# Two FNO attention layers on one core: one mixing of the images per pass, and every unit of work issued in one written-out order

## The chip, the cores and the metric

One core of a Trainium2 chip. TensorE (PE in the profile) multiplies, VectorE (DVE), ScalarE (ACT) and GpSimd (POOL) do elementwise work, and SyncE (SP) issues transfers. The metric is the time of one launch in microseconds on the device.

## The reference

The input is `x` of shape (2, 56, 128, 128): two images b of 56 channel planes each. Two layers of the same form follow each other, `x = x + layer(gn(x))`. Cut to what matters:

```python
xn = inorm(xa)                                  # xa: 112 single planes
k, q, v = (spectral_conv(xn, w) + skip1x1(xn)) for 8 heads each
attn = softmax(q k^T / 128, over the 56 planes of the image)
out  = spectral_conv(attn v) + skip1x1(attn v)  # heads folded to one plane
att  = inorm(out + xa)
h = gelu(inorm(spectral_conv(inorm(att))) + skip(...))
h = inorm(spectral_conv(h)) + skip(h)
y = inorm(h) + att
```

`spectral_conv` keeps 2 x 16 rows by 16 columns of the 2-D Fourier transform. Planes stay 128 x 128. Scores, values and heads are therefore computed among 512 modes per plane, and only three things touch whole planes: the statistics and transforms of the input, the hidden image under the Gelu, and the output. The part of every layer that is linear and pointwise is a 56 x 56 mixing of the raw planes of an image.

## The kernel before, in words

Both images' raw planes are held in `X2` (128 partitions: 56 planes twice, for two interleaved halves of the rows, plus pad partitions). For each layer L and image b a pass has these steps:

- `turned` (lines 356 to 373): a unit of 8 row pairs is transposed by TensorE into a pair of PSUM banks (L363 in layer 0, L365 in layer 1, there on 120 partitions at once), copied out by ACT (L368, L371) into the plane tile `P[b]`, and DVE takes `bn_stats` (L373). Eight units make an image.
- `modes_chain` (L458 on): group statistics, `Sqrt` on ACT (L468), reciprocal, then the plane is scaled and shifted in place (L479 on ACT, L481 on DVE) before the Fourier matmuls (L485) and `to_modes` (L386). A transfer over SP's queue moves half of the modes to other partitions (L505).
- `gram` (L521), `gram_chain`, `scale_x` (L560: `X2` times the group scale, in place, DVE alone), `scores` (L607, L588), `softmax_chain`, `values` (L630), `mix_chain` (the 56 x 56 mixing matrix `BTx`), `heads` (L700).
- `norms_chain`: closed-form norms (Sqrt on ACT, L731), the spectrum `Z` of the hidden image, and two scaled copies of the mixing matrix, `Bs` and `Be`.
- `gelu`: for each of four parts A of an image, `synthesis` (L761) of the spectrum into two PSUM pairs and `mixed` (L776, with `Bs`) on top of it; ACT applies the Gelu (L829), DVE takes `bn_stats` (L831), TensorE transposes (L811), ACT copies (L812), forward transform (L799), DVE copy (L804).
- `h_chain`: four in-place DVE transposes (L845), `to_modes`, norms (Sqrt, L869, L876), spectrum of the output.
- `end`: for each part synthesis and `mixed` again (L776, with `Be`); DVE adds the hidden image (L926), POOL adds the raw image (L928), which SP's queue loaded again (L906); in layer 0 the sum goes to `X2` and to a DRAM tile `store`, and is turned for layer 1; in layer 1 it goes to `out`.

The order of the work is written by generators: each step is a generator that yields an estimated cost, and `_woven(lead, *bulks)` fills the waits of a chain of small steps (the lead) with units of another image's bulky step. PSUM comes from two pools, two single banks (`bank`) and three pairs (`pair`), taken in turn. The framework (Tile) makes each engine's order from this one, and may set an instruction ahead of an earlier one; an engine then works through its instructions in order and waits by semaphores.

`prepare` (L235 on) makes coefficient matrices from the weights: for layer 0 first on DVE and POOL (`prepare(0, V, G)`), for layer 1 on POOL. `relay` and `build` (L341) spread them into the tiles `WU`, `WT`, `WM`.

Of the kernel before, what the change touches and what calls it, by code (L numbers as in the profile page):

```python
# [16 lines left out]
HEADS = 8  # L44
EPS = 1e-5

# [3 lines left out]
for _name, _n in (  # L50
    ("ident", N), ("fw", 32), ("fh", N), ("gw", N), ("group", N), ("dup", N), ("ext", N), ("fold", 64),
    ("raw", 56), ("count", 2), ("syn", 1), ("same", 32), ("m8", 8), ("m16", 16), ("n2", 1), ("fx", N), ("gh", 2 * N),
):
    _PARTS[_name] = (sum(n for _, n in _PARTS.values()), _n)
N_CONST = sum(n for _, n in _PARTS.values())


def _constants():
# [9 lines left out]
    at = 4 * (pos % 32) + pos // 32  # L68
    fh = over_h(at)[0]
    g, s, e, c = at // 16, at // 8 % 2, at // 2 % 4, at % 2  # L70
    by_layer = []
    for hx, hz in (
        (16 * g + 8 * c + 4 * s + e, pos.reshape(4, 4, 2, 4).transpose(1, 0, 3, 2)),
        (16 * g + 4 * c + 8 * s + e, pos.reshape(4, 2, 4, 4).transpose(2, 0, 3, 1)),
    ):
        z = over_h(hz.reshape(-1))[1]
        by_layer += [over_h(hx)[0], np.concatenate([z, z], 0).reshape(N, 2 * N)]
# [7 lines left out]
    for r in range(2):  # L85
# [20 lines left out]
        "ident": np.eye(N), "fw": fw, "fh": fh, "gw": gw, "group": group, "dup": dup, "ext": ext,  # L106
        "fold": fold, "raw": raw,
# [7 lines left out]
    whole = np.concatenate([parts[n] for n in _PARTS if n in parts] + by_layer, 1)  # L115
    return {"all": np.ascontiguousarray(whole, np.float32)}

# [23 lines left out]
def _woven(lead, *bulks):  # L141

    rest = chain(*bulks)
    for want in lead:
        while want > 0:
            cost = next(rest, None)
            if cost is None:
                break
            yield cost
            want -= cost  # L150
    yield from rest


def _with(bulk, extra):

    for cost in bulk:
        next(extra, None)
        yield cost


def _run(units):
    for _ in units:
        pass
# [3 lines left out]
def fno_layers(ctx: ExitStack, tc: tile.TileContext, x, out, weights, small, const):  # L167
    nc = tc.nc
    V, S, G, T = nc.vector, nc.scalar, nc.gpsimd, nc.tensor
    pool = lambda name, bufs, **kw: ctx.enter_context(tc.tile_pool(name=name, bufs=bufs, **kw))  # L170
    cp = pool("const", 1)
    xp = pool("x", 1)
    pp = pool("plane", 1)
    wp = pool("mats", 1)
    sp = pool("modes", 1)
    sm = pool("small", 1)
    dp = pool("dram", 1, space=bass.MemoryType.DRAM)
    ps = pool("psum", 2, space=bass.MemoryType.PSUM)
    pq = pool("pair", 3, space=bass.MemoryType.PSUM)

    def bank():
        return ps.tile([N, 512], F32, name="bank")

    def pair():
        return pq.tile([N, 2, 512], F32, name="pair")

    def little(name, shape):
        return sm.tile(shape, F32, name=name)
# [3 lines left out]


    Ct = cp.tile([N, N_CONST], F32, name="C")
    C = {k: Ct[:, o : o + n] for k, (o, n) in _PARTS.items()}
    ident = C["ident"]
    nc.scalar.dma_start(out=ident, in_=const["all"][:, :N])
    stage = cp.tile([N, 1632], F32, name="stage")
    nc.scalar.dma_start(out=stage[:, :1088], in_=weights[0].rearrange("p m r n t -> p (m r n t)"))
    smt = [cp.tile([N, N_SMALL], F32, name=f"sm{n}") for n in range(2)]  # L200
    for n in range(2):
        nc.scalar.dma_start(out=smt[n], in_=small[n : n + 1, :].to_broadcast([N, N_SMALL]))
    nc.scalar.dma_start(out=Ct[:, N:], in_=const["all"][:, N:N_CONST])
    X2 = xp.tile([N, B, 64, N], F32, name="X2")
    xin = x.rearrange("b k (g c r) w -> c b k g (r w)", c=2, r=8)
    for b in range(B):
        for g in range(0, 8, 2):
            for c in range(2):
                nc.sync.dma_start(
                    out=X2[64 * c : 64 * c + K, b, 8 * g : 8 * g + 16, :].rearrange("p (g r) w -> p g (r w)", r=8),  # L210
                    in_=xin[c, b, :, g : g + 2, :],
                )
    for b in range(B):
        nc.sync.dma_start(out=X2[K:64, b], in_=x[b, :8, :64, :])
    eps = cp.tile([N, 1], F32, name="eps")
    V.memset(eps, EPS)
    ones = cp.tile([N, N], F32, name="ones")
    V.memset(ones, 1.0)
    P = [pp.tile([N, 8192], F32, name=f"P{b}") for b in range(B)]
    plane = [t[:, : N * K].rearrange("p (i k) -> p i k", i=N) for t in P]  # L220
    WU = wp.tile([N, 4096], F32, name="WU")
    WT = wp.tile([N, 4096], F32, name="WT")
    WM = wp.tile([N, 1024], F32, name="WM")
# [5 lines left out]
    hT = [WT[:, 2048 + 896 * j : 2944 + 896 * j].rearrange("p (r e c k) -> p r e c k", r=2, e=4, c=2) for j in range(2)]  # L229
    xr = cp.tile([N, 3, 1024], F32, name="xr")  # L230
    G.memset(xr.rearrange("p a b -> p (a b)"), 0.0)
    store = dp.tile([B, K, N, N], F32, name="store")


    def prepare(layer, first, second):  # L235

        sml = smt[layer]
# [6 lines left out]
        der = little(f"der{layer}", [N, 48])  # L244
# [8 lines left out]
        tt, ts = second.tensor_tensor, second.tensor_scalar  # L253
        ss, vp = col("ss", 8), col("vp", 8)
        tt(ss, par["s_q"], par["s_k"], ALU.mult)
        tt(vp, par["s_p"], par["s_v"], ALU.mult)
        g2 = col("g2")
        tt(g2, par["g1"], par["g1"], ALU.mult)
        ts(col("score_g", 8), ss, g2, 1.0 / N, ALU.mult, ALU.mult)
        ts(col("mix", 8), vp, par["g1"], None, ALU.mult)  # L260
        tt(col("A0"), par["g2"], par["gan"], ALU.mult)
        tt(col("A02"), d["A0"], d["A0"], ALU.mult)
        tt(col("A0m0"), d["A0"], par["m0sw"], ALU.mult)
        ts(col("gan2"), par["gan"], par["gan"], EPS, ALU.mult, ALU.add)
        ts(col("dc0"), par["m0sw"], par["b2"], par["m0sb"], ALU.mult, ALU.add)
        tt(col("bb"), par["ban"], par["bmo"], ALU.add)
        tt(col("gm1"), par["gmo"], par["m1sw"], ALU.mult)
        tt(col("m12"), par["m1sw"], par["m1sw"], ALU.mult)
        tt(col("m2"), par["m1sw"], par["m1sw"], ALU.add)
        first.tensor_tensor(Wf, Wf, _bc(rawc[:, 0], 1, 2 * N_W), ALU.mult)  # L270
        first.tensor_tensor(M, M, _bc(rawc[:, 1:3], 2, N_W), ALU.mult)
        first.tensor_tensor(W, W, M, ALU.add)
        first.tensor_tensor(W[:, 0, 0:32, :], W[:, 0, 0:32, :], _bc(sml[:, 0:32], 2, 8), ALU.add)
# [5 lines left out]
        def place(e, t64, to, re, im, k):  # L279
# [4 lines left out]
            e.tensor_tensor(u, re, m0, ALU.mult)  # L284
            e.tensor_tensor(v, im, m1, ALU.mult)
            e.tensor_tensor(to[:, :, 0], u, v, ALU.subtract)
            e.tensor_tensor(u, im, m0, ALU.mult)
            e.tensor_tensor(v, re, m1, ALU.mult)
            e.tensor_tensor(to[:, :, 1], u, v, ALU.add)

        def product(e, room, o, a, b, conj, minus, scale, k):
            t64 = [room[:, 64 * n : 64 * n + 64].rearrange("p (a t) -> p a t", a=8) for n in range(4)]
            re, im, u = t64[:3]
            e.tensor_tensor(re, part(0, a), part(0, b), ALU.mult)
            e.tensor_tensor(u, part(1, a), part(1, b), ALU.mult)
            e.tensor_tensor(re, re, u, ALU.add if conj else ALU.subtract)
            e.tensor_tensor(re, re, _bc(minus, 2, 8), ALU.subtract)
            e.tensor_tensor(im, part(0, a), part(1, b), ALU.mult)
            e.tensor_tensor(u, part(1, a), part(0, b), ALU.mult)
            e.tensor_tensor(im, im, u, ALU.subtract if conj else ALU.add)  # L300
            for t in (re, im):
                e.tensor_scalar(t, t, scale, None, ALU.mult)
            place(e, t64, cpt[:, o : o + 16].rearrange("p (a c) t -> p a c t", c=2), re, im, k)
            return t64

        product(first, rooms[0], 0, 1, 0, True, ss, g2, 3)
        t64 = product(second, rooms[1], 16, 3, 2, False, vp, par["g1"], 5)
        place(
            second, t64, cpt[:, 32:36].rearrange("p (n c) t -> p n c t", c=2), W[:, 0, 32:34, :], W[:, 1, 32:34, :], 5,
        )  # L310
        tcs = little("tc", [N, 8, 36])
        return par, d, cpt, tcs

    def relay(cpt, tcs, room, groups):

        L = room.rearrange("p (t e c j s) -> p t e c j s", t=8, e=2, c=2, j=4)
        for o, n in groups:
# [17 lines left out]
            S.copy(tcs[:, :, o : o + n], pt[:, : 8 * n].rearrange("p (t n) -> p t n", t=8))  # L335
            yield 0.0

    def build(to, tcs, o, ts):

# [695 lines left out]
```

## Time and profile before

| | us |
|---|---|
| runs of the kernel before | 554.09, 555.94 (median), 558.58 |
| span of the profiled execution (one of its own; the page gives no total time for it) | 548.9 |
| PE busy | 440.6 |
| DVE busy | 350.6 |
| ACT busy | 189.6 |
| POOL busy | 180.4 |

A row of the groups reads: line, engine, operation, output tile from input tiles, partitions by elements, count, then busy time of the group in us and the mean of one in ns, then the idle time of the engine just before these instructions with what ended it. A row of the stretches gives, for a stretch from A to B us, the busy time of each engine with the count of instructions, the granted TensorE clock as a share of full speed, the busy share of the DMA engines and the rate in GB/s. A row of the timeline or of the chain begins with start and duration in us.

### The profile page before, as it was taken

Reading aid. Unit: us, or ns where it says so; the run is one execution under the profiler, and the core shown is the slowest. Engines: PE = TensorE matmul, PEld = TensorE weight load, DVE = VectorE, ACT = ScalarE, POOL = GpSimd, SP = SyncE. Lnnn points to the kernel's source line nnn. Section 1 sums busy time; section 2 is a strip of 40 time slices with the busy share of each in tenths; the row PEclk is TensorE's granted clock in tenths of the full one; section 3 lists DMA queues with packets and bytes.
Section 4 is the critical chain, followed back from the end, with each engine's and each line's share of the span. In section 5 each row is a group of like instructions: output and inputs, shape, how many; then the busy total and the mean of one; then the engine's idle time right before and its main releaser. Section 6 shows DMA issues by size and latency. Waiting matters only on the chain.

```text
span 548.9 us, 14430 instructions
## 1 busy us (share of the span) xinstructions
PE 440.6 (80%) x6438; PEld 296.4 (54%) x6438; DVE 350.6 (64%) x593; ACT 189.6 (35%) x238; POOL 180.4 (33%) x198
## 2 busy tenths in 40 slices
PE   2548879899989999789688948899998999977480
PEld 1423748768675555445563447577775555534340
DVE  0575579934547676869459994761636867767670
ACT  2333232064545557142102313224546457502000
POOL 2460325900082000155366771440000000044484
PEclk9998797999998999996667958989998999979696
DMA  8992000050000000065144641121000000027597
GB/s 209 220 221 28 10 2 11 7 148 3 2 3 1 1 2 1 1 198 172 51 132 117 187 116 32 13 69 41 4 1 2 1 1 3 1 60 225 181 219 289
DMA packets 18477, 41.00 MB, mean 75 GB/s; under 512 B 4704, under 2 KB 5472, under 8 KB 18400
## 3 DMA queue, kind: packets, MB, share of 16 engines
q1 hardware_dynamic: 17696, 38.71, 26.0%
q10 hardware_dynamic: 720, 1.38, 1.0%
q8 instruction: 50, 0.82, 0.6%
q14 instruction: 11, 0.09, 0.1%
HBM read 24.68 MB, written 14.68 MB: 72 GB/s over the span
## 4 chain that ended last, share of the span: by engine, by line
PE 46%; DVE 30%; ACT 8%; issue 7%; POOL 4%; DMA 3%; POOLq 1%; ACTq 0%; DVEq 0%
PE pair L776 8%; PE pair L761 5%; PE pair L811 5%; DVE X L560 4%; DVE stats L373 4%; PE bank L521 4%; PE bank L700 3%; DMA C<-const_all 3%; DVE P L926 3%; PE bank L485 3%; PE bank L588 3%; PE bank L799 2%; DVE WT L406 2%; PE bank L386 2%; POOL P L928 2%
## 5 line engine op out<-in xcount | busy, mean ns | idle before, releaser
L926 DVE SCALAR_TENSOR_TENSOR P<-P,hs,pair 128x1024 f32<-128x1024 f32 x32 | 40.0, 1268 | 18.8 <-PE pair L776 18.8
L831 DVE BATCH_NORM_STATS2 stats<-P 128x6 f32<-128x512 f32 x64 | 40.5, 680 | 17.3 <-ACT P L829 17.1
L928 POOL TENSOR_TENSOR X<-P,xr 128x1024 f32<-128x1024 f32 x16 | 39.3, 2462 | 32.1 <-DVE P L926 20.2
L373 DVE BATCH_NORM_STATS2 stats<-P 128x6 f32<-128x448 f32 x64 | 35.7, 612 | 20.9 <-ACT P L371 10.6
L560 DVE TENSOR_TENSOR X<-X,gvr 120x1024 f32<-120x1024 f32 x32 | 49.0, 1560 | 0.0
L829 ACT ACTIVATE P<-pair 128x1024 f32<-128x1024 f32 x32 | 32.6, 1026 | 33.0 <-PE pair L776 32.4
L521 PE MATMUL bank<-P 128*64 128x56 f32 (+1 forms) x1024 | 40.5, 250 | 0.0
L776 PE MATMUL pair<-X,Be 57*64 57x512 f32 x256 | 40.1, 726 | 0.0
L521 PEld LDWEIGHTS bank<-P 128*64 128x64 f32 (+1 forms) x1024 | 38.9, 164 | 2.2 <-issue 1.9
L395 POOL MEMSET WT<- 128x256 f32 x4 | 1.3, 314 | 114.5 <-PE bank L799 88.8
L811 PEld LDWEIGHTS pair<-C,P 120*128 120x128 f32 x256 | 27.3, 145 | 21.3 <-issue 11.5
L776 PE MATMUL pair<-X,Bs 57*64 57x512 f32 x256 | 38.4, 641 | 0.0
L761 PE MATMUL pair<-C,WT 32*128 32x128 f32 x512 | 29.3, 336 | 11.1 <-DVE P L926 5.3
L761 PEld LDWEIGHTS pair<-C,WT 32*128 32x128 f32 x512 | 24.0, 229 | 23.4 <-issue 9.3
L811 PE MATMUL pair<-C,P 120*128 120x120 f32 x256 | 35.2, 281 | 0.1
L341 POOL TENSOR_TENSOR WT<-tc,C 128x1024 f32<-128x1024 f32 x8 | 26.5, 3343 | 20.1 <-ACT tc L335 11.0
L812 ACT COPY WT<-pair 128x896 f32<-128x896 f32 x32 | 28.8, 905 | 11.8 <-PE pair L811 11.5
L363 PE MATMUL pair<-C,X 56*128 56x56 f32 x256 | 17.4, 291 | 17.5 <-DMA X<-x 11.9
L371 ACT COPY P<-pair 128x896 f32<-128x896 f32 x16 | 14.4, 901 | 45.7 <-PE pair L365 45.7
L363 PEld LDWEIGHTS pair<-C,X 56*128 56x128 f32 x256 | 14.9, 197 | 24.0 <-DMA X<-x 10.0
L365 PE MATMUL pair<-C,X 120*128 120x120 f32 x128 | 20.3, 312 | 9.2 <-POOL X L928 9.2
L365 PEld LDWEIGHTS pair<-C,X 120*128 120x128 f32 x128 | 16.1, 163 | 21.2 <-POOL X L928 11.6
(260 smaller groups left out, 880.2 us busy)
## 6 DMA issues: line engine op xcount, KB each, us to landing
X<-x SPq DMA_DIRECT2D x16, 448.0 KB
xr<-x SPq DMA_DIRECT2D x32, 224.0 KB
store<-X SPq DMA_DIRECT2D x32, 224.0 KB
out<-P SPq DMA_DIRECT2D x32, 224.0 KB
xr<-store SPq DMA_DIRECT2D x16, 224.0 KB
X<-store SPq DMA_DIRECT2D x16, 224.0 KB
C<-const_all ACTq DMA_DIRECT2D x1, 618.0 KB
stage<-weights ACTq DMA_DIRECT2D x1, 544.0 KB
```

The source lines that it names most:

```text
L363: T.transpose(p[:, c, o : o + K], X2[q, b, i, :], ident[q, q], tile_position=(64 * c, 0))
L365: T.transpose(p[:, s, N * e : N * e + 120], X2[:120, b, i, :], ident[:120, :120])
L373: V.bn_stats(stats[:, 2 * g + s, :], dst[:, 448 * s : 448 * s + 448])
L521: T.matmul(p[u : u + m, :K], lhsT=P[b][:, K * i : K * i + m], rhs=plane[b][:, i, :], start=(i < 2), stop=(i == N - 1), tile_position=(0, u ...
L560: V.tensor_tensor(v, v, _bc(st["gvr"][:120], 1, 8), ALU.mult)
L761: T.matmul(both[j // 2][:, j % 2, N * e : N * e + N], lhsT=Z[32 * j : 32 * j + 32, o : o + N], rhs=C["gw"][32 * j : 32 * j + 32, :], start ...
L776: T.matmul(p[64 * c : 64 * c + 64, r, :], lhsT=Bs[q, :], rhs=X2[q, b, s : s + 4, :].rearrange("p e w -> p (e w)"), start=False, stop=True, ...
L811: T.transpose(p[:, r, N * e : N * e + 120], h3[:120, o : o + N], ident[:120, :120])
L829: S.activation(h3, both[v].rearrange("p r m -> p (r m)"), AF.Gelu)
L831: V.bn_stats(stats[:, 4 * A + 2 * v + r, :], h3[:, 512 * r : 512 * r + 512])
L926: V.scalar_tensor_tensor(h3, h3, st["hs"], both[v].rearrange("p r m -> p (r m)"), ALU.mult, ALU.add)
L928: G.tensor_tensor(dst, h3, back(n), ALU.add)
```

## The change

- **The way of issuing.** No call reaches an engine at once. A `Work` object records units (one instruction, or a group that stays together): 1304 of them. Each unit knows the engines that may run it. `ORDER` lists for each place the unit (as a difference to the one before) and a letter for the engine (V DVE, S ACT, G POOL, T PE, Q SP); `PLACES` gives the PSUM bank of each of 324 allocations, in one tile of eight banks. The units are issued inside `tc.manual_schedule()`, in which the framework keeps the given order and still places the semaphores. Units of several passes interleave: units of the second image's Gelu stand among those of the first's hidden chain, those of layer 1's modes among layer 0's output.
- **The mixing.** The raw planes are mixed once per pass, in `gelu`, with `BTx` unscaled. DVE adds the mixed image times one column of scales to the raw image and puts the sum over `X2`; then the synthesis is accumulated on the mixed image in PSUM, and the Gelu takes the other scale as its `scale`. `end` has the synthesis alone, then DVE's sum, then the add of `X2` on POOL or DVE. The raw image is loaded again in `gelu` (32 transfers from `x`, 32 from `store`), not in `end`.
- **Statistics of the hidden image**: `Square` on ACT with a running sum, writing back into PSUM, in place of `bn_stats` on DVE.
- **Modes**: the transform matrix is scaled (`fwg`) and the shift enters as a one-row matmul (`crow`); the plane is scaled later, for the Gram alone. Copies from PSUM replace the transfer of L505, and the transposes of L845 read PSUM part by part, so that `to_modes` becomes 64 matmuls with 32 rows in `h_chain`.
- **Roots**: `pow` with -0.5 on POOL in place of `Sqrt` on ACT and a reciprocal on DVE (24 times).
- **Turning**: both layers in the form of L363. `scale_x` on POOL (22 of 32) or DVE (10).

```diff
-def _woven(lead, *bulks):
-    rest = chain(*bulks)
...
+class Work:
+    def issue(self, engines, order):
+        for n, letter in order:
+            for choices in self.units[n][1]:
+                method, args, kw = choices[letter]
+                getattr(engines[letter], method)(*args, **kw)
...
+    def banks(n):
+        work.taken.append(n)
+        k = PLACES[len(work.taken) - 1]
+        return psum[:, k : k + n, :]
...
+    def root(to, of):
+        tt("G", to, of, mhalf[: of.shape[0], : of.shape[1]], ALU.pow)
...
 gelu:
+                moved(L, xr[:, n % 3], n, b, None, raw, False, "QS")
+                with work.unit():
+                    for c in range(2):
+                        s = 8 * n + 4 * c
+                        for r in range(2):
+                            q = slice(64 * r, 64 * r + K + 1)
+                            T.matmul(both[v][64 * c : 64 * c + 64, r, :], lhsT=st["BTx"][q, :], ...)
+                base = X2[:, b, 8 * n : 8 * n + 8, :].rearrange("p e w -> p (e w)")
+                V.scalar_tensor_tensor(
+                    base, both[v].rearrange("p r m -> p (r m)"), cols[:, 1:2], xr[:, n % 3], ALU.mult, ALU.add,
+                )
+            synthesis(A, both, st["Z"], False)
...
-                    S.activation(h3, both[v].rearrange("p r m -> p (r m)"), AF.Gelu)
-                    for r in range(2):
-                        V.bn_stats(stats[:, 4 * A + 2 * v + r, :], h3[:, 512 * r : 512 * r + 512])
+                S.activation(h3, both[v].rearrange("p r m -> p (r m)"), AF.Gelu, scale=cols[:, 0:1])
+                S.activation(
+                    both[v].rearrange("p r m -> p (r m)"), h3, AF.Square, scale=1.0 / N, accum_out=sqs[:, n : n + 1],
+                )
...
 end:
-                mixed(L, b, A, v, both[v], st["Be"])
                 V.scalar_tensor_tensor(h3, h3, st["hs"], both[v].rearrange("p r m -> p (r m)"), ALU.mult, ALU.add)
-                G.tensor_tensor(dst, h3, back(n), ALU.add)
+                tt("GV", dst, h3, base, ALU.add)
...
+    with tc.manual_schedule():
+        work.issue({"V": nc.vector, "S": nc.scalar, "G": nc.gpsimd, "T": nc.tensor, "Q": nc.sync}, decoded(ORDER))
```

All instructions of the changed kernel carry the line of the recording call (L212), so its groups are told apart by tiles and shapes.

More of the change, by code (lines that the diff above doesn't have):

```diff
@@ L195, in fno_layers, with move @@
+    def move(who, to, of):
+        work.call({c: ("dma_start", (), dict(out=to, in_=of)) for c in who})
+    Ct = hold("C", [N, N_CONST])
     C = {k: Ct[:, o : o + n] for k, (o, n) in _PARTS.items()}
     ident = C["ident"]
[L197 to L200, printed above, removed]
@@ L307, in prepare @@
[L307 to L314, printed above, removed]
[L316 to L329 removed]
+                ts(who, t, t, scale, None, ALU.mult)
@@ L474, in modes_chain @@
+        root(gv, var)
+        V.scalar_tensor_tensor(sh, gs[:, 0:1], -1.0, gv, ALU.mult, ALU.mult)
+        fwg = hold(f"fwg{b}", [N, 32])
+        V.tensor_scalar(fwg, C["fw"], gv, None, ALU.mult)
+        p = bank()
+        T.matmul(p[0:1, :32], lhsT=sh, rhs=C["fw"], start=True, stop=True)
+        crow = hold(f"crow{b}", [1, 32])
+        copy("SV", crow, p[0:1, :32])
         wide = P[b][:, 7168 : 7168 + N]
+        copy("GV", wide, gv.to_broadcast([N, N]))
+        for c in range(2):
+            ts("GV", wide[:, 64 * c + K : 64 * c + K + 1], sh, -1.0, None, ALU.mult)
@@ L510, in modes_chain, with gram @@
+        for j in range(4):
+            v = P[b][:, 1792 * j : 1792 * j + 1792]
+            affine("SV", v, v, gv, sh)
         p = bank()
-        T.matmul(p[:, :N], lhsT=wide, rhs=ident, start=True, stop=True)
-        gvr = little(f"gvr{b}", [N, N])
-        S.copy(gvr, p[:, :N])
+        T.transpose(p[:, :N], wide, ident)
+        gvr = hold(f"gvr{b}", [N, N])
+        copy("SV", gvr, p[:, :N])
         st.update(xf=xf, xs=xs, gvr=gvr)
-    def gram(b, st):
+    def gram(L, b, st):
+        work.note = f"gram{L}{b}"
@@ new lines, in norms_chain @@
+        pc = bank()
+        T.matmul(pc[:, :2], lhsT=C["dup"][:K, :], rhs=r02, start=True, stop=True)
+        cols = hold(f"cols{b}", [N, 2])
+        copy("VS", cols, pc[:, :2])
+        p = bank()
+        sums(p, 0, sqy, True, True, left[:, K : 2 * K])
+        tm = hold(f"tm{b}", [K, 1])
+        with work.unit():
+            V.tensor_scalar(tm, p[:K, 0:1], d["A02"][:K], None, ALU.mult)
+            V.scalar_tensor_tensor(k3[:, 2:3], k3[:, 1:2], EPS, tm, ALU.mult, ALU.add)
+        root(rs[:, 2:3], k3[:, 2:3])
```

1262 lines of the change are left out of this document (673 added, 589 removed).

## The prediction

> **What bounds the kernel now.** I read the page's totals first, then the slices, then the busy time of each engine in seven stretches cut where the stages change.
>
> ```profile
> span 548.9 us, 14430 instructions
> PE 440.6 (80%) x6438; PEld 296.4 (54%) x6438; DVE 350.6 (64%) x593; ACT 189.6 (35%) x238; POOL 180.4 (33%) x198
> ...
> PE   2548879899989999789688948899998999977480
> ...
> PEclk9998797999998999996667958989998999979696
> ...
> GB/s 209 220 221 28 10 2 11 7 148 3 2 3 1 1 2 1 1 198 172 51 132 117 187 116 32 13 69 41 4 1 2 1 1 3 1 60 225 181 219 289
> ```
> ```profile
> core 0: us, PE busy (x) PEld busy (x) DVE busy (x) ACT busy (x) POOL busy (x), PEclk, DMA share, GB/s
> 0.00:62.00 62.00, 31.32 (x315) 19.86 (x315) 30.12 (x74) 20.61 (x23) 18.18 (x67) 0.96 0.67 152
> 62.00:157.00 95.00, 86.00 (x1760) 69.96 (x1763) 59.12 (x94) 31.51 (x45) 36.56 (x27) 0.92 0.11 26
> 157.00:226.00 69.00, 64.46 (x774) 37.75 (x777) 51.25 (x101) 40.12 (x47) 11.37 (x40) 0.98 0.01 1
> 226.00:345.00 119.00, 94.18 (x1063) 61.17 (x1063) 88.82 (x123) 27.45 (x36) 61.02 (x39) 0.76 0.41 116
> 345.00:414.00 69.00, 63.49 (x1349) 49.85 (x1344) 33.84 (x62) 26.57 (x37) 14.99 (x9) 0.98 0.10 26
> 414.00:483.00 69.00, 64.45 (x778) 37.83 (x772) 50.66 (x99) 39.73 (x47) 0.99 (x2) 0.98 0.01 2
> 483.00:549.00 66.00, 36.72 (x436) 20.00 (x428) 36.83 (x44) 3.58 (x7) 37.29 (x16) 0.79 0.66 202
> ```
>
> TensorE leads in every stretch but the last, where DVE and POOL stand level with it. It idles 30.7 us of the first 62, then 9.0, 4.5, 24.8, 5.5 and 4.5 us (48.3 together), then 29.3 us of the last 66: 108.3 us. So span = 440.6 us of PE work + 108.3 us without it, and the sum below changes these two. It is made against the span of 548.9 us. The page has no total time for that execution; the median of the runs, 555.94 us, is 7.0 us longer, and I add those.
>
> **PE work.** The rows it is priced from (busy us of the group, mean ns of one; one matmul issues two instructions, a transpose one):
>
> ```profile
> L776 PE MATMUL pair<-X,Be 57*64 57x512 f32 x256 | 40.1, 726 | 0.0
> L776 PE MATMUL pair<-X,Bs 57*64 57x512 f32 x256 | 38.4, 641 | 0.0
> L811 PE MATMUL pair<-C,P 120*128 120x120 f32 x256 | 35.2, 281 | 0.1
> L607 PE MATMUL pair<-xf,WU 64*64 64x56 f32 x1024 | 22.4, 228 | 0.0
> L485 PE MATMUL bank<-P,C 128*32 128x448 f32 x128 | 21.1, 675 | 7.2 <-DVE P L481 6.8 <-ACT P L479 0.2 <-DVE WT L490 0.2
> L365 PE MATMUL pair<-C,X 120*128 120x120 f32 x128 | 20.3, 312 | 9.2 <-POOL X L928 9.2
> L700 PE MATMUL bank<-P 128*64 128x56 f32 x512 | 18.9, 224 | 0.0
> L363 PE MATMUL pair<-C,X 56*128 56x56 f32 x256 | 17.4, 291 | 17.5 <-DMA X<-x 11.9 <-DMA C<-const_all 5.5
> L386 PE MATMUL bank<-WU,C 128*64 128x448 f32 x32 | 6.9, 552 | 0.0
> ```
>
> - Mixing once instead of twice: 256 of 512 instructions go, half of 40.1 + 38.4 us: -39.3.
> - Transposes: 128 of L365 (20.3) become 256 of L363's shape (17.4), 256 of L811 (35.2) become 512 of it (34.8): -3.3.
> - The spectrum of the hidden image: 32 instructions (6.9 us) become 512 narrow ones of 112 columns on 32 rows. One costs between 0.022 us (L607) and 0.057 us (the synthesis, quoted below, on as few rows): 11 to 29 us. I take L700's 0.037, as its output is as tall: 18.9, or +12 (+4 to +22).
> - The shift of the mean, now a one-row matmul: 32 instructions at L485's 0.165: +5.3, and 1 for its row.
> - The input's spectrum is 64 short matmuls in place of 16 long ones with the same columns: 0.
>
> Net -24.3. The groups overlap (the page's rows add up to about a tenth more than 440.6), so -22. Then the clock: the stretch 226 to 345 ran at 0.76 with PE idle for 21% of it; the stretch 62 to 157, idle for 9%, at 0.92. Filled like that, its 94.2 us shrink by 94.2 x (1 - 0.76/0.92) = 16; I take -15, with 0 and -20 (at 0.98) as ends. PE after: 440.6 - 22 - 15 = 404. The Trainium skill, "TensorE: Matmul & The Clock Gate", Part 1, states that the clock halves after an idle window of about 3.4 us and is else full; by that a filled stretch would save 94.2 x 0.24 = 23, and the sum would come 8 us lower. The row at 0.92, filled but not full, is why I don't take it.
>
> **The other engines.** None may pass PE, so each gets a ledger.
>
> ```profile
> L560 DVE TENSOR_TENSOR X<-X,gvr 120x1024 f32<-120x1024 f32 x32 | 49.0, 1560 | 0.0
> L831 DVE BATCH_NORM_STATS2 stats<-P 128x6 f32<-128x512 f32 x64 | 40.5, 680 | 17.3 <-ACT P L829 17.1
> L926 DVE SCALAR_TENSOR_TENSOR P<-P,hs,pair 128x1024 f32<-128x1024 f32 x32 | 40.0, 1268 | 18.8 <-PE pair L776 18.8
> L928 POOL TENSOR_TENSOR X<-P,xr 128x1024 f32<-128x1024 f32 x16 | 39.3, 2462 | 32.1 <-DVE P L926 20.2 <-DVE gs L465 4.4 <-DVE stats L373 3.0
> L829 ACT ACTIVATE P<-pair 128x1024 f32<-128x1024 f32 x32 | 32.6, 1026 | 33.0 <-PE pair L776 32.4
> L761 PE MATMUL pair<-C,WT 32*128 32x128 f32 x512 | 29.3, 336 | 11.1 <-DVE P L926 5.3 <-DVE WT L406 4.1 <-DVE mv L461 1.4
> L341 POOL TENSOR_TENSOR WT<-tc,C 128x1024 f32<-128x1024 f32 x8 | 26.5, 3343 | 20.1 <-ACT tc L335 11.0 <-PE bank L386 9.1
> L845 DVE STREAM_TRANSPOSE WU<-WU 128x448 f32<-128x448 f32 x16 | 14.9, 1012 | 0.1
> L804 DVE COPY WU<-bank 128x448 f32<-128x448 f32 x16 | 9.8, 612 | 9.2 <-PE bank L799 9.2
> L829 ACT ACT_TABLE_LOAD x6 | 7.7, 1283 | 2.9 <-PE pair L776 2.8
> L495 POOL TENSOR_SCALAR P<-sh 128x1 f32<-128x1 f32 x8 | 5.1, 650 | 0.4
> ```
>
> DVE: 22 of 32 scalings go to POOL (-34), the Gelu statistics go (-40.5), L804 goes (-9.8); added are 32 fused raw-plus-mixed sums, priced as L926 (+40.6), 23 wide PSUM copies taken from ACT at up to 2 x 0.612 (+27) and five final adds (+7): 341. ACT: 32 Squares, priced as the Gelu (+33), 16 of 20 table loads gone in the built program (-20.5), 23 copies gone (-21): 181. It also issues 62 transfers, where it issued five; a Gelu queued behind an image load waits with it until that buffer is free, and ACT has 404 - 181 us to spare for that. POOL: +22 x 2.46 for scalings, five adds fewer (-12), 24 small powers: 180 + 54 - 12 + 24 x 0.65 = 238. SP loses 83 issues (164 to 81), the small gathers among them. DMA bytes hardly change: the images are read again beside the Gelu units and not at the end, and the slices between 7 and 15 carry almost nothing, so there is room. Costed at nothing: scaling the planes (now a whole-row operation after the spectrum, needed by the Gram alone, with the spectrum's matmuls as cover), the shuffled half of the modes (two copies out of PSUM where a transfer through SP's queue stood), and clearing of pad columns (made once). If that cover were gone they would cost what their rows say, about 1.2 us a plane part and 0.6 a copy. All stay under PE's 404.
>
> **Time without PE work.** At the start, DVE holds the statistics of image 0 behind a preparation that waits for constants:
>
> ```profile
> 19.77 0.73 DVE L270 TENSOR_TENSOR stage<-stage,C 128x544 f32<-128x544 f32 x1 [18.61 <-DMA C<-const_all]
> ...
> 25.98 8.00 DVE L373 BATCH_NORM_STATS2 stats<-P 128x6 f32<-128x448 f32 x15
> ...
> 36.84 1.21 DVE L481 TENSOR_SCALAR P<-P,gv,sh 128x1792 f32<-128x1792 f32 x1
> ```
>
> The preparation moves to POOL, and image 0's Gram and scores no longer come after all of image 1's turning. Its first power still stands behind the preparation on POOL: the weights come after six image transfers and constants, 3.5 MB at the 215 GB/s of the first slices, 16 us and 3 of lead, and 24 small POOL steps (under L495's 0.65 each, say 11 us) follow. So I expect the modes at about 30 instead of 36.8 us. I take -10 of 30.7 (0 to -15). Middle: where two passes meet (226 to 345) I take off half of 24.8, elsewhere a third of 23.5: -20 (0 to -25). Only unit-by-unit interleaving of several passes can do this; which waits remain is what I know least.
>
> The tail, from the last Gelu unit on, is the hidden chain and then the output:
>
> ```profile
> 516.40 3.22 DVE L406 STREAM_TRANSPOSE WT<-pair 128x896 f32<-128x896 f32 x2 [1.97 <-PE pair L401]
> ...
> 523.51 18.52 POOL L928 TENSOR_TENSOR P<-P,X 128x1024 f32<-128x1024 f32 x8 [5.61 <-DMA X<-store]
> ```
>
> Three of four L845 transposes run earlier (-3), L804's last copy goes (-0.6), the narrow spectrum matmuls add 3, eight adds of 18.5 us on POOL become DVE's 8 x 1.27 + 3 x 1.2 = 13.8 (-4.7), mixing of the other image leaves PE's queue (-4), a table load goes (-1.3): 66 becomes 55. PE has 16 mixing units fewer in it (16 x 1.23 = 20) and 3 us more spectrum, so 20 of work; idle 35 instead of 29.3: +6.
>
> Idle after: 108.3 - 10 - 20 + 6 = 84. Span 404 + 84 = 488; time **495 us**.
>
> **Rivals.**
> - *Faster rates.* In quiet places the same groups run quicker than their means:
>
> ```profile
> 165.12 1.02 PE pair L776 x8
> ...
> 171.67 1.10 PE pair L761 x32
> ```
>   0.128 against 0.153 us, and 0.034 against about 0.057. If an order without collisions gets these everywhere: 256 x 0.025 + 1024 x 0.02 = 27 less: 468. Against it: means hold inside full stretches too.
> - *PSUM held longer.* The mixed image stays in its banks while DVE reads it, the synthesis is added, and Gelu and Square run: 2 x 1.02 + 2 x 1.27 + 1.10 + 4 x 1.03 = 9.8 us for four of eight banks, where mixing, synthesis and Gelu took 5.2. Synthesis now waits for DVE, with PE's later units queued behind it. There are 16 such halves (four to an image and layer). If no two ever overlap, 16 x 9.8 = 157 us, against the 138 us of the two Gelu stretches (157 to 226, 414 to 483), which also hold a hidden chain's few us of PE: about +22, 517. For it: transposes need two banks more and the forward step one, so a second half can't be held whole. Against it: only mixing and synthesis of the next half need its banks, and the order may put them last.
> - *POOL paces the scaling.* Mixing an image needs its scaled tiles; 22 of them take 2462 ns (L928) where DVE took 1560 (L560): if each were waited for, +22 x 0.9 = 20, 515. Against it: POOL is busy 238 of 488 us, and the tiles are due only after Gram, scores, values and softmax of their image. The Trainium skill, "GPSIMD Engine Reference", section 4.1, has the same rule, that elementwise work belongs on VectorE, with GpSimd about twice as slow on two inputs; the trace's ratio is 1.6.
> - *The order does nothing.* Idle stays 108.3 and the clock too: 440.6 - 22 + 108.3 = 527, 534 us. A fixed order that misjudges durations stalls whole queues.
> - *Slower: the power on POOL.* No row shows it. Each replaces a table load (1.28), a square root and a reciprocal; I take 0.65 (L495), between nothing and 3.34 (L341, the dearest POOL row). All 24 stand in chains; uncovered, they decide from 0.65 + 61/24 = 3.2 us each on. At 4.0: 495 + 80 = 575.
>
> **How the numbers follow.** Forecast 0.52, faster rates 0.15, PSUM 0.09, POOL's scaling 0.05, order does nothing 0.10, power 0.09. Of the order that does nothing, 0.03 lies within 1% of before (a measurement here can tell about 1%). So faster 0.88, same 0.03, slower 0.09. The range 460 to 540 leaves out the last rival and the outer edges of the faster rates and of the order that does nothing, under 0.2 together.
>
> **What would show it.** Right: PE near 404 us at a clock above 0.92 past 200 us; four table loads; the first Gram before 45 us; about 55 us after the last Gelu. Wrong: powers above 2 us each with PE waiting for POOL; synthesis waiting long for DVE's sums; the spectrum's narrow matmuls at 0.057 us or more; PE idle still above 100 us.

## The result, and the profile after

The changed kernel took 541.1 us in the median of four runs (532.9 to 551.5), the kernel before 557.3 on the same chip. Two of the four, over 1.5% longer than the fastest, are left out of the ratio: 0.960 of the time before (95%: 0.951 to 0.970), some 535 us. A second set gave 535.8 us and 0.960 again (0.955 to 0.965). It is faster by 4%; forecast were 495 us, 11%. The profiled execution took 539.5 us, with a span of 537.4.

First the totals of the page, and PE's busy share and granted clock in 40 equal slices, in tenths, as they were shown of the kernel before:

```profile
span 537.4 us, 15963 instructions
...
PE 400.1 (74%) x7194; PEld 293.5 (55%) x7194; DVE 368.8 (69%) x551; ACT 175.2 (33%) x242; POOL 261.0 (49%) x243
...
PE   0069976978949779789668868576998789896460
...
PEclk9999978586979788978656798968899989957555
```

PE works 400.1 us, close to the 404 of the sum, and stands 137.3 us without work, where the sum had 84. To see where, the span is cut at the same events in both kernels: the first Gram, the first and last Gelu or Square of each layer. Busy time by stretch, before and then after (columns: PE, PEld, DVE, ACT, POOL, granted clock, DMA share, GB/s):

```profile
0.00:62.70 62.70, 32.02 (x317) 20.54 (x317) 30.82 (x75) 21.07 (x23) 18.18 (x67) 0.96 0.66 150
62.70:159.00 96.30, 87.31 (x1796) 70.60 (x1796) 59.80 (x95) 31.63 (x45) 38.56 (x33) 0.92 0.11 25
159.00:217.40 58.40, 55.46 (x659) 31.99 (x655) 42.91 (x88) 36.79 (x43) 9.35 (x33) 0.97 0.01 2
217.40:415.40 198.00, 166.08 (x2503) 116.18 (x2503) 130.90 (x198) 56.79 (x76) 76.70 (x49) 0.84 0.28 79
415.40:473.90 58.50, 55.55 (x662) 32.15 (x658) 41.96 (x85) 36.91 (x43) 0.01 (x1) 0.97 0.01 2
473.90:548.90 75.00, 44.23 (x523) 24.94 (x521) 44.24 (x56) 6.39 (x12) 37.60 (x17) 0.82 0.59 178
```
```profile
0.00:56.50 56.50, 25.63 (x320) 19.39 (x320) 23.50 (x54) 13.46 (x15) 27.75 (x72) 1.00 0.87 192
56.50:174.40 117.90, 96.48 (x1861) 73.68 (x1863) 68.84 (x108) 23.54 (x33) 89.61 (x93) 0.81 0.09 18
174.40:237.00 62.60, 51.81 (x863) 32.04 (x855) 42.31 (x69) 45.08 (x64) 2.67 (x6) 0.88 0.34 87
237.00:409.30 172.30, 135.94 (x2589) 104.50 (x2589) 135.68 (x193) 46.12 (x65) 105.53 (x53) 0.80 0.19 55
409.30:475.40 66.10, 58.77 (x1073) 38.72 (x1072) 48.13 (x76) 43.55 (x61) 2.31 (x4) 0.92 0.32 86
475.40:537.40 62.00, 31.45 (x510) 25.15 (x508) 50.32 (x55) 3.43 (x9) 33.17 (x15) 0.58 0.40 119
```

Stretch less PE busy gives PE's idle time (the last column is the combined kernel of the experiments):

| us of PE idle | before | after | combined |
|---|---|---|---|
| start, to the first Gram | 30.7 | 30.9 | 26.7 |
| attention of layer 0 | 9.0 | 21.4 | 8.8 |
| Gelu of layer 0 | 2.9 | 10.8 | 9.6 |
| between the Gelus | 31.9 | 36.4 | 28.2 |
| Gelu of layer 1 | 3.0 | 7.3 | 7.5 |
| tail | 30.8 | 30.6 | 30.2 |
| sum | 108.3 | 137.3 | 111.0 |

Where POOL is busiest for the length of the stretch, idle has grown most: in the attention of layer 0 POOL went from 38.6 to 89.6 us, and the stretch from 96.3 to 117.9. Groups of POOL and DVE in the changed kernel (busy us, mean ns):

```profile
L212 POOL TENSOR_TENSOR X<-X,gvr 128x1024 f32<-128x1024 f32 x22 | 60.7, 2773 | 12.5 <-issue 7.1 <-ACT gvr L212 4.4 <-DMA X<-const_ones 1.0
L212 POOL TENSOR_TENSOR rr<-rr,mhalf 128x57 f32<-128x57 f32 x4 | 37.9, 9464 | 11.3 <-DVE rr L212 11.3
...
L212 POOL TENSOR_TENSOR f<-f,mhalf 56x1 f32<-56x1 f32 x4 | 2.2, 541 | 76.1 <-DVE f L212 76.1
```
```profile
L212 DVE TENSOR_TENSOR X<-X,gvr 128x1024 f32<-128x1024 f32 x10 | 22.6, 2288 | 2.6 <-DMA X<-const_ones 2.4 <-ACT gvr L212 0.2
```

Twenty powers are of one or two columns, at 0.5 to 0.7 us; four, in the Gram's chains, are of 128x57 elements and last 9.46 us each. What one does (timeline of the changed kernel; in brackets the idle time before, and its releaser):

```profile
340.57 9.46 POOL L212 TENSOR_TENSOR rr<-rr,mhalf 128x57 f32<-128x57 f32 x1
350.00 0.54 POOL L212 TENSOR_TENSOR gv<-var,mhalf 128x1 f32<-128x1 f32 x1
350.50 2.34 POOL L212 TENSOR_TENSOR X<-X,gvr 128x1024 f32<-128x1024 f32 x1
350.57 2.37 DVE L212 TENSOR_SCALAR fwg<-C,gv 128x32 f32<-128x32 f32 x1 [8.06 <-POOL gv L212]
...
352.99 1.72 PE L212 MATMUL psum<-P,fwg 128*32 128x448 f32 x8 [8.94 <-DVE fwg L212]
```

The other image's modes wait behind it for a power of 0.54 us; then a 128x32 scaling on DVE (2.37 us) ends with POOL's scaling and not before, where the same step lasted 0.29 us at 42.01; PE loses 8.94 us.

### The profile page after: what moved, and what is told of

It reads as the page before. It is cut to its first block, busy times and chain, and to the rows that moved or that the text cites. A ratio compares the mean times of both kernels' runs of the same rounds, so it can differ in the third digit from the quotient of the medians.

```text
span 537.4 us, 15963 instructions
## 1 busy us (share of the span) xinstructions
PE 400.1 (74%) x7194; PEld 293.5 (55%) x7194; DVE 368.8 (69%) x551; ACT 175.2 (33%) x242; POOL 261.0 (49%) x243
## 5 line engine op out<-in xcount | busy, mean ns | idle before, releaser
L212 ACT COPY P<-psum 128x896 f32<-128x896 f32 (+5 forms) x65 | 55.0, 861 | 130.1 <-PE psum L212 111.9
L212 PE MATMUL psum<-P 128*64 128x56 f32 (+1 forms) x1632 | 67.2, 241 | 6.5 <-DVE P L212 5.3
L212 PEld LDWEIGHTS psum<-P 128*64 128x64 f32 x1632 | 59.7, 150 | 13.3 <-DVE P L212 4.8
L212 POOL TENSOR_TENSOR X<-X,gvr 128x1024 f32<-128x1024 f32 x22 | 60.7, 2773 | 12.5 <-issue 7.1
L212 PE MATMUL psum<-C,P 56*128 56x56 f32 (+4 forms) x1124 | 55.2, 269 | 10.8 <-DVE X L212 5.0
L212 PEld LDWEIGHTS psum<-C,P 56*128 56x128 f32 (+4 forms) x1124 | 45.3, 173 | 31.6 <-issue 11.9
L212 DVE SCALAR_TENSOR_TENSOR X<-psum,cols,xr 128x1024 f32<-128x1024 f32 x32 | 40.4, 1273 | 18.7 <-PE psum L212 12.7
L212 PE MATMUL psum<-C,X 56*128 56x56 f32 x512 | 27.7, 279 | 32.3 <-DMA X<-x 27.5
L212 DVE BATCH_NORM_STATS2 stats<-P 128x6 f32<-128x448 f32 x64 | 35.4, 610 | 13.7 <-ACT P L212 13.6
L212 PEld LDWEIGHTS psum<-C,X 56*128 56x128 f32 x512 | 24.8, 188 | 36.2 <-DMA X<-x 27.6
L212 PE MATMUL psum<-C,WT 32*128 32x128 f32 (+1 forms) x528 | 32.2, 356 | 15.1 <-DVE P L212 12.1
L212 POOL TENSOR_TENSOR rr<-rr,mhalf 128x57 f32<-128x57 f32 x4 | 37.9, 9464 | 11.3 <-DVE rr L212 11.3
L212 POOL TENSOR_TENSOR P<-P,X 128x1024 f32<-128x1024 f32 x13 | 32.2, 2498 | 19.9 <-DVE c L212 14.8
L212 ACT ACTIVATE P<-psum,cols 128x1024 f32<-128x1024 f32 x32 | 34.8, 1108 | 19.9 <-PE psum L212 18.7
L212 DVE SCALAR_TENSOR_TENSOR P<-P,hs,psum 128x1024 f32<-128x1024 f32 x32 | 39.2, 1270 | 2.4 <-PE psum L212 2.4
L212 DVE STREAM_TRANSPOSE P<-psum 128x448 f32<-128x448 f32 (+1 forms) x24 | 28.6, 1211 | 16.0 <-PE psum L212 14.4
L212 POOL TENSOR_TENSOR f<-f,mhalf 56x1 f32<-56x1 f32 x4 | 2.2, 541 | 76.1 <-DVE f L212 76.1
L212 PEld LDWEIGHTS psum<-C,WT 32*128 32x128 f32 (+1 forms) x528 | 27.6, 251 | 20.5 <-DVE P L212 14.8
L212 PE MATMUL psum<-X,BTx 57*64 57x512 f32 x256 | 35.8, 625 | 3.2 <-ACT psum L212 2.6
L212 POOL TENSOR_TENSOR X<-P,X 128x1024 f32<-128x1024 f32 x14 | 34.7, 2505 | 6.8 <-DVE P L212 6.8
L212 ACT ACTIVATE psum<-P 128x1024 f32<-128x1024 f32 x32 | 32.9, 1028 | 1.1 <-issue 0.4
L212 PE MATMUL psum<-P,fwg 128*32 128x448 f32 x128 | 21.5, 780 | 11.2 <-DVE fwg L212 11.2
```

What stands on the lines that cost most here:

```text
L212: getattr(engines[letter], method)(*args, **kw)
```

## The experiments

Theory: the lost 53 us come from three things at their own places: the wide power, the order of the first loads, and wide POOL work that holds DVE up. Rival: whatever is mended, a fixed order only shows its next wait. Ratios are to the kernel before on the same chip, the changed kernel being at 0.960; intervals are at 95%.

**The wide power.** The power is taken of the column, ahead of the matmuls that spread it:

```diff
+            V.tensor_scalar(vc, vc, EPS, None, ALU.add)
+            root(vc, vc)
...
+            V.tensor_scalar(vd, ident[:K, :K], vc, None, ALU.mult)
             T.matmul(p[:, :K], lhsT=ones[:K, :], rhs=vd, start=True, stop=True)
...
-        V.tensor_scalar(rr, p[:, : K + 1], EPS, None, ALU.add)
-        root(rr, rr)
+        V.tensor_copy(rr, p[:, : K + 1])
```

> The power of the Gram's chain is taken of the 56x1 column on GpSimd before it is spread by the two matmuls, in place of the 128x57 matrix after them; everything else, the order too, as in the changed kernel. Theory (the four wide powers of 9.46 us each are a part of the 137 us without PE work): the four powers cost about 0.55 us each, POOL's busy time falls from 261 to about 225 us, the gaps of 8.94 us at 353 and 6.75 us at 156 go, PE idle falls by 15 to 30 us and the time from 541 to 512-526 us. Rival (POOL is off the path, or the order's next wait takes the place): POOL falls by the same 36 us and the time by less than 6 us.

540.7 us, 0.970 (0.964 to 0.977): POOL fell to 225.2 us, and the time not at all (the ratio is a point higher). DVE had risen from 368.8 to 388.7. The first of the four chains, with the new 56x56 operation on DVE:

```profile
74.51 0.57 POOL L213 TENSOR_TENSOR vc<-vc,mhalf 56x1 f32<-56x1 f32 x1 [4.41 <-DVE vc L213]
...
75.42 5.21 DVE L213 TENSOR_SCALAR vd<-C,vc 56x56 f32<-56x56 f32 x1
75.95 4.63 POOL L213 TENSOR_TENSOR X<-X,gvr 128x1024 f32<-128x1024 f32 x2
```

It lasts 5.21 us and ends when two of POOL's scalings end (75.95 + 4.63 = 80.58). So the operation goes to ACT in the next form:

```diff
-            V.tensor_scalar(vd, ident[:K, :K], vc, None, ALU.mult)
+            S.activation(vd, ident[:K, :K], AF.Copy, scale=vc)
```

> The narrow power again, but the 56x56 diagonal of it is written by ACT and not by DVE, where it lasted 0.9 to 8.0 us beside POOL's scalings (in the first form POOL fell from 261.0 to 225.2 us as it should, DVE rose from 368.8 to 388.7, and the time did not fall). Theory (DVE's operations with both operands in SBUF are held to the end of a wide POOL operation, and that ate the gain): DVE back at 365-372 us, POOL at 225, the diagonal under 0.4 us on ACT, the time 10 to 20 us below the first form's (541 to 521-531). Rival (the narrow power only brings the next wait of the fixed order): DVE falls the same and the time stays within 5 us of 541.

520.3 us, 0.931 (0.924 to 0.938). The operation takes 0.34 us on ACT:

```profile
L213 ACT ACTIVATE vd<-C,vc x4: 340/341/342, 73.3 to 376.2; 56x56 f32<-56x56 f32 x4
```

Moving four small operations from DVE to ACT, in the same places, is worth 4 points, 22 us; PE's waits for the tile `vd` fall from 23.5 to 3.9 us. Against the changed kernel the narrow power gains 3 points, 16 us, with 35.7 us less POOL work.

**The scalings.** `scale_x` on DVE throughout, places unchanged:

```diff
+MOVED = {182: 'V', 176: 'V', 181: 'V', ...}
...
-decoded(ORDER)
+[(n, MOVED.get(n, c)) for n, c in decoded(ORDER)]
```

> All 32 scalings of the image by the norm run on DVE (22 of them ran on POOL); places in the order as in the changed kernel. Theory (DVE's wide operations on SBUF stretch to the end of a wide POOL operation beside them): DVE's own scalings fall from a mean of 2.29 to 1.2-1.6 us and DVE gains only about 22 x 1.2 minus 15 to 25 us of lost stretching, so its busy time goes from 369 to 372-385, POOL from 261 to about 200; PE idle falls by 5 to 15 us. Rival (DVE becomes crowded, the stretching costs nothing on the path): DVE rises to 395 or more, PE idle rises, and the time is 5 to 15 us longer.

528.1 us, 0.950 (0.944 to 0.956); POOL 205.5, DVE 371.0, PE idle 125.6 us.

```profile
L212 DVE TENSOR_TENSOR X<-X,gvr 128x1024 f32<-128x1024 f32 x32 | 41.3, 1308 | 1.4 <-DMA X<-const_ones 0.9 <-ACT gvr L212 0.4
```

DVE took over 22 scalings and was busy 2 us longer: each costs 1308 ns with no scaling on POOL, 2288 beside them. The theory holds, though the one point gained is at the edge of what can be told.

**The first loads.** Transfers and turned tiles change places, image 0 first:

```diff
-        out.append((last, word[-1]))
+        out.append((LOADS.get(last, last), word[-1]))
```

> The twenty transfers of the start keep their places in the two queues but the eight of image 0 and the first constants take the first places of both, the weights and image 1 the later ones, and the turning of image 0 goes in the order in which its pieces come; all else as in the changed kernel. Theory (the late start is the order of the loads): the first transposes start at 6 to 10 us where they start at 25.6, the first modes at 28 to 33 where they are at 39.8, PE idle and the time fall by 8 to 15 us (541 to 526-533). Rival (the modes wait for the preparation on POOL and the later constants anyway): the transposes start early too, but the first Gram stays within 3 us of 56.5 and the time within 4 us of 541.

532.1 us, 0.958 (0.952 to 0.964), no gain that can be told from 0.960. The changed kernel's first matmuls, then those of this one, and its ACT queue:

```profile
25.62 4.15 PE L212 MATMUL psum<-C,X 56*128 56x56 f32 x65 [25.62 <-DMA X<-x]
```
```profile
6.05 0.35 PE L212 MATMUL psum<-C,X 56*128 56x56 f32 x1 [6.05 <-DMA C<-const_all]
...
23.78 5.37 PE L212 MATMUL psum<-C,X 56*128 56x56 f32 x112 [11.18 <-ACT P L212]
```
```profile
11.03 10.47 ACTq L212 DMA_DIRECT2D X<-x  x4
21.52 1.28 ACT L212 ACT_TABLE_LOAD   x1 [21.52 <-DMA sm<-small]
22.82 1.72 ACT L212 COPY P<-psum 128x896 f32<-128x896 f32 x2
```

PE starts at 6 us, then waits 11.2 for ACT, which stands behind ten transfers in its own queue until 21.5. (The table load names `sm` as its releaser, but it starts when the issue of four image transfers ends, at 11.03 + 10.47 us.) The first matmul of the modes, on the statistics `mv`, comes at 34.2 in place of 39.8.

**Together.** First the two that had gained nothing, then loads and scalings, then all three (the power in its second form).

> The narrow power and image 0 first together. Theory (both are separate waits at separate places): the gains add, 541 to 500-517 us, PE idle from 137 to 95-115 us, and the granted clock rises from 0.82 to 0.85 or more where the gaps close. Rival (each only uncovers the next wait of a fixed order): less than two thirds of the sum of the single gains. A clock that stays at 0.82 or lower with less idle time would say that the clock does not follow the gaps.

534.2 us, 0.962 (0.957 to 0.966): nothing again; the held DVE operation is still in it.

> The changed kernel once more, beside the three that follow on the same chip, since its first four times spread from 532.9 to 551.5. Both theories: a ratio to before of 0.955 to 0.97. Below 0.955 the gains seen so far of the scaling on DVE (0.950) and of image 0 first (0.958) are smaller than they look; the narrow power (0.970) is then a loss.

535.8 us, 0.960 (0.955 to 0.965).

> Image 0 first, and all scalings on DVE, together; wide power as in the changed kernel. Theory (two separate waits at separate places; alone they gave 532.1 and 528.1 against 541 for the changed kernel): 517 to 524. Rival (each only uncovers the next wait): 526 or more.

521.9 us, 0.938 (0.933 to 0.943): 2.2 points, where the two gained 0.2 and 1.0 alone. Beside the scalings the order of the loads is worth 1.2 points (0.950 to 0.938).

> Image 0 first, all scalings on DVE and the narrow power with its diagonal on ACT. Theory: no POOL operation over 2.5 us is left in the chains of the Gram; POOL 165-170 us, DVE 368-374, PE idle 100-115 us, time 500 to 514. Rival (the order's places, not its durations, hold PE): PE idle stays above 120 us and the time above 520.

504.0 us, 0.903 (0.898 to 0.909), faster than both kernels. PE idle 111.0 us, POOL 169.8. By stretch (cut as above):

```profile
0.00:52.20 52.20, 25.51 (x318) 18.61 (x318) 23.26 (x54) 13.28 (x15) 27.23 (x72) 0.84 0.84 215
52.20:149.80 97.60, 88.80 (x1863) 70.00 (x1863) 74.33 (x123) 23.89 (x36) 40.67 (x80) 0.91 0.08 18
149.80:211.30 61.50, 51.95 (x861) 32.44 (x855) 42.34 (x69) 45.09 (x64) 2.65 (x6) 0.87 0.35 89
211.30:371.70 160.40, 132.21 (x2592) 101.70 (x2591) 131.72 (x204) 46.38 (x67) 63.73 (x44) 0.84 0.20 60
371.70:441.40 69.70, 62.16 (x1071) 40.31 (x1071) 48.20 (x77) 43.56 (x61) 2.31 (x4) 0.85 0.30 81
441.40:503.20 61.80, 31.62 (x508) 25.65 (x508) 50.28 (x55) 3.38 (x8) 33.20 (x15) 0.58 0.40 120
```

The attention of layer 0 and the stretch between the Gelus give back 20.8 of the 26.3 us. Gelu and tail are as before the mending.

**The two halves of the change apart.** The second mixing is given back (with weights of zero), then the order is loosened:

```diff
 def synthesis
+            for v in range(2 if fresh else 0):
...
+                        T.matmul(both[v][64 * c : 64 * c + 64, r, :], lhsT=kept["zero"][q, :], ...)
```
```diff
-    with tc.manual_schedule():
+    if True:
```

> The changed kernel with the second mixing given back to TensorE: ahead of the synthesis of each part of the output stand the 8 matmuls a tile that the kernel before had there, on the image's tile, with a weight of zeros (they add nothing; the result is the same). Order, engines and banks as in the changed kernel. It adds 256 matmuls of 0.14 us (35.8 us in the group of the mixing). Theory (in this order PE is not what most stretches wait for, since it idles 137 us): half of the output stages stand in the tail, where PE has 30 idle us, so the time grows by 8 to 22 us. Rival (PE's work is the bound, as the prediction's sum has it): PE busy and the time grow alike, by 30 to 40 us, to the time of the kernel before or more.

545.4 us, 0.986 (0.979 to 0.994): mixing once is worth 2.6 points, 14 us. The added matmuls are 34.2 us in their group; PE busy rises by 19.2 us to 419.3 and PE idle falls by 12.5 to 124.8 (against the repeat of the changed kernel by 30.8 and 16.4). The granted clock was 0.86 with the weights of zero, 0.82 and 0.84 without them, so the price may be low; no run has other weights.

> The same units, engines and banks, listed in the same order, but the framework may set an instruction ahead of an earlier one, as it could in the kernel before. Theory (the waits come from durations and queues at a few places and the strict places are worth little by themselves): within 15 us of 536. Rival (the exact places of the searched order carry the gain): 20 us longer or more. A shorter time by over 5 us would say that the strict order itself costs.

594.3 us, 1.074 (1.063 to 1.085): the rival's. Both PE's work (430.2 us) and its idle time (163.8) grow.

```profile
PE psum L212 <- DVE P L212: 57.9, 24, 17.5
```

PE waits 57.9 us for DVE's writes to `P` (31.2 in the strict order). Held strictly, the order is worth 11 points against the same list loosened.

**What was left.** ACT's queue was cleared of the later loads, then of the stores too, by more entries in the same list:

```diff
+MOVED: 14: 'Q', 16: 'Q', 18: 'Q', 20: 'Q'
+MOVED: 524: 'Q', 1036: 'Q', 539: 'Q', ...
```

> The kernel with image 0 first, scalings on DVE and the narrow power, and four transfers of image 1 issued from SP's queue where they stood in ACT's, ahead of ACT's first copies (there the last four lasted 10.8 us in ACT's queue, and ACT's first copy of a turned tile began at 23.1 us, with PE waiting 11.5 us for it). Theory (a transfer that its queue can't take yet holds the engine that issues it): ACT's first copy at 11 to 14 us, the gap of 11.5 us falls below 4, the time falls by 4 to 10 us from 504. Rival (the start is bound by the arriving image and the weights): first copy early too, but the modes start within 2 us of where they did and the time stays within 3 us.

508.9 us, 0.911 (0.900 to 0.922), no gain, as the rival had it. ACT copies from 12.4 us on, but in PE's queue a turned tile of image 1 stands ahead of image 0's modes, and its pieces now come by one queue: PE waits 5.83 us for them, until 41.33, and the Fourier matmuls of the modes start at 42.4, where the combined kernel had them at 37.1.

> As the kernel before it in this list, and the 20 transfers to and from the stored image that ACT issues between the two layers and in layer 1's Gelu are issued by SP as well (in ACT's queue a copy of the spectrum stood 18.3 us behind them, with PE waiting 6.2 us). Theory: that gap goes, PE idle falls by 5 to 10 us and the time by 3 to 10 us more. Rival (SP's queue then holds the loads that Gelu needs behind the stores): waits for the raw image's tile take its place, and the time is equal or longer.

510.6 us, 0.923 (0.916 to 0.929), not better. The spectrum's copy no longer waits for a store (16.8 us before, on ACT); waits of PE for DVE's transposes in `WT` rose from 2.6 to 6.7 us.

> The kernel with image 0 first, scalings on DVE and the narrow power, once more, as the base of the two that follow. Every theory: a ratio to before of 0.895 to 0.915.

503.5 us, 0.905 (0.900 to 0.910): the base of the last two. In the first of them the output of the Square goes to SBUF:

```diff
-                    both[v].rearrange("p r m -> p (r m)"), h3, AF.Square, ...
+                    WU[:, 3584:4096].bitcast(mybir.dt.bfloat16), h3, AF.Square, ...
```

> The base with the output of the Square (which nobody reads; only its running sum is used) written to a free piece of SBUF in 16 bits and not back over the two PSUM banks, so that these come free after the Gelu and not after the Square. Theory (PSUM held longer keeps PE waiting in the Gelu stretches): PE's waits for ACT's writes to PSUM (7.0 us in the base) fall below 2, PE idle in the two Gelu stretches falls from 17 to 10-13 us, the time by 3 to 7 us. Rival (those small waits are ACT's pace, which the Square sets either way): the waits change their name and the time stays within 2 us.

503.3 us, 0.906 (0.901 to 0.912), the same. PE's 7.5 us of waits for ACT's writes to PSUM are gone; its waits for ACT's writes to `P` go from 11.6 to 14.5 us and for DVE's to `WT` from 2.6 to 6.6.

Last, the 14 adds of layer 0's output that POOL made go into the list, as 'V':

> The base with the 14 adds of layer 0's output that POOL makes (2.5 us each) on DVE (1.3 us when POOL is quiet). Theory (what POOL still holds up between the layers is worth more than DVE's added 18 us): POOL 135, DVE 380-388, PE idle between the layers falls from 28 to 18-24 us, time 4 to 8 us shorter. Rival (DVE, busy 132 of 160 us in that stretch, becomes the bound there): the time grows by 2 to 12 us.

507.9 us, 0.915 (0.909 to 0.920): a point slower than the base, at the edge of what can be told. DVE is busy 141.0 of the 161.7 us between the Gelus, more than PE (133.3), which fits the rival, that DVE becomes the bound there.

## Why the prediction was wrong

**PE's work: the total right by luck, the terms not.** The rows after:

```profile
L212 PE MATMUL psum<-X,BTx 57*64 57x512 f32 x256 | 35.8, 625 | 3.2 <-ACT psum L212 2.6 <-ACT WT L212 0.4 <-ACT xf L212 0.2
...
L212 PE MATMUL psum<-C,X 56*128 56x56 f32 x512 | 27.7, 279 | 32.3 <-DMA X<-x 27.5 <-ACT xf L212 4.0 <-POOL X L212 0.3
L212 PE MATMUL psum<-C,P 56*128 56x56 f32 x512 | 27.2, 253 | 2.8 <-ACT psum L212 2.3 <-DVE vd L212 0.5
...
L212 PE MATMUL psum<-WU,C 32*64 32x112 f32 x512 | 9.5, 296 | 0.8 <-ACT psum L212 0.8
L212 PE MATMUL psum<-crow,C 1*32 1x448 f32 x32 | 3.8, 546 | 0.0
```

Mixing -42.7 (forecast -39.3). Transposes from 72.9 to 54.9, -18.0 (forecast -3.3: the 56-row form was priced from a row taken during the start's loads, 0.068 us, and costs 0.054). Hidden spectrum +2.6 (forecast +12). Shift +3.8 (+5.3). Together these are -54.3, and all the groups of PE -45.8 (479.6 to 433.8), so the rest, whose work was to stay the same, came out 8.5 us longer. The 404 was met because more work went than forecast and what was left took longer than forecast. The -15 for a better clock did not come: 0.82 after, 0.89 before. With the waits mended it was 0.83 to 0.84, with PE idle down by 26 us, so "filled like that" was no rule. That mixing once is worth only 14 us of time says that PE's work was not all of the bound either.

**Time without PE work: this step failed.** Expected were -10 at the start, -20 in the middle, +6 in the tail; measured (by the table) 0, +29 and 0. The length of the tail was right: 13 us shorter, forecast 11 (from a cut a little later). Its terms were not: PE worked 31.5 us in it, where 20 were forecast, and idled 30.6, where 35 were.

- *Start*: the prediction had the images arrive at 215 GB/s and the statistics follow. It left out that each queue mixed both images and that ACT's first copies stand in ACT's queue behind transfers. The first Gram came at 56.5 us; before 45 was the prediction's sign. With image 0 first the modes come 5.6 us earlier, with ACT's queue still in the way; with that cleared too, PE waits for POOL's preparation (2.25 us) and image 1 (5.83) instead. The time gained alone is too small to tell.
- *Middle*: two prices. The power was taken at 0.65 us each with 3.34 as the end of its range; 20 of 24 cost that, but four are wide, and at 128x57 they cost almost three times the dearest row it was bounded by. The diff shows `rr` at K + 1 columns; the sum counted 24 equal powers. And the ledgers ("None may pass PE", "POOL is busy 238 of 488 us") set busy time against busy time, while POOL holds DVE up: the scalings were thought to be taken off DVE at 1560 ns each, and DVE got its ten others at 2288, with small steps of the chains stretched as well. DVE came to 368.8 us in place of 341. The Trainium skill, "SBUF — State Buffer", section "Who interferes with whom", states it: a DVE operation with two inputs in SBUF contends with a GpSimd operation that reads SBUF, as does a `tensor_scalar` in a two-port mode, and the one that issues second waits for the whole of the first; one with at most one SBUF input, outside those modes, does not contend. The rows agree: 5.21 us for 56x56 beside POOL, and 1273 and 1270 ns for DVE's sums with one operand in PSUM. Of the Trainium skill the prediction weighed only "GPSIMD Engine Reference", section 4.1, that GpSimd is about twice as slow on two inputs, and it priced the wrong engine.
- *Tail*: the same hold stands here, and no run lifted it. A 56x1 product on DVE (`f<-f,r`) lasts 4.13 us from 497.98 and ends when two of POOL's adds end (497.46 + 4.64 = 502.10); the same product lasts 0.15 us at 475.01. It is as long in the combined kernel (4.13 us from 464.22). What it costs stays open.

The wide power, the loads and the scalings, mended, take back 26 us of idle time (31 in the repeat). That leaves PE idle at 106 to 111 us, as in the kernel before. The filling itself gave nothing: from the first Gram to the last Gelu the combined kernel idles 54.1 us, the one before 46.8. That is the rest of the gap to 84, and its cause stays open. The combined kernel is faster than the one before by its 48 us less PE work alone (440.6 to 392.3).

**The rivals.** *The power on POOL* named the mechanism for four of the 24; at +16 us, not the 80 that would have made it slower. *POOL paces the scaling* had the right place and the wrong victim. *PSUM held longer*: the Gelu stretches idle 12 us more (forecast 22), but freeing the banks earlier brought nothing, so the cause of these 12 stays open. *The order does nothing* gave 534, near what came, for a wrong reason: it kept idle at 108.3 us, and 137.3 came. Loosened, the same list costs 11 points, so the strict order does much for this list.

**Open**: the clock. The tail ran at 0.58 with PE busy 31.5 of 62.0 us; with the mixing given back, more densely:

```profile
475.00:544.10 69.10, 46.27 (x666) 26.39 (x662) 50.72 (x64) 5.26 (x10) 34.13 (x17) 0.75 0.36 107
```

The Gelu stretches fell from 0.97 to 0.88 and 0.92 as their idle share rose from 5% to 17% and 11%. But the start ran at 1.00 with PE idle more than half of it (in the combined kernel at 0.84, in its repeat at 1.00, idle about as much), and the whole span hardly faster (0.83) with 26 us less idle time. The Trainium skill, "TensorE: Matmul & The Clock Gate", Part 1, lets the clock halve after an idle window; the tail and the Gelu stretches agree with it in direction, the start does not, and no run here shows the window.

## What to carry to other kernels

Before moving work to an engine that has time to spare, ask what its operations share with the engine that has none: here 22 scalings moved to POOL saved DVE 2 us of busy time and cost about 1 point (6 us), or 2 (11 us) once the first loads were mended. Price a new operation at the size at which each call runs it, and count calls by shape. In a fixed order, look at what stands behind each long instruction and each transfer in the same queue, since that is what a wrong duration costs.

## What the runs showed of the hardware

- `pow` on POOL: 0.54 us for 56x1, 0.70 for 56x2, 9.46 for 128x57: about 0.16 us for each column more ((9.46 - 0.54) / 56).
- A 56x56 `tensor_scalar` on DVE lasted 0.9 to 8.0 us beside POOL's scalings; as an activation on ACT 0.34 in all four places.
- ACT's first compute stood until 21.5 us behind ten transfers issued in its own queue, though the tile that it copied had been turned by 12.6 us; with the last four of them issued by SP, it started at 11.1 us.
